# Self attention of a decoder layer: the denominators of all four head groups summed on VectorE, the last group finished inside the output projection, and one feed-forward block moved to the last cross attention

## The chip, the cores and the metric

The kernel runs on one core of one Trainium2 chip. The metric is the device time of one execution in microseconds (us); the figure quoted is the median of three runs. The engines are called TensorE (PE in the profile, PEld for its weight loads), VectorE (DVE), ScalarE (ACT), GpSimd (POOL) and SyncE (SP, which issues the DMAs). TensorE writes its results into PSUM; everything else lies in SBUF.

## What is computed

The reference is one pre-norm decoder layer on four batches of 512 tokens with 512 features, 16 heads of 32, all in float32:

```python
x = x + attn(layernorm(x), q_w, q_b, k_w, k_b, v_w, v_b, o_w, o_b)   # causal self attention
x = x + xattn(layernorm(x), ctx, ctx)     # causal, raw queries, keys and values, no weights
x = x + ffn(layernorm(x), W_up, W_down, W_gate, W_expert)
```

Both attentions are a softmax over the earlier positions. The feed-forward part is `relu(f @ W_up.T) @ W_down.T` plus `f @ W_expert` times the sum of a softmax over the two largest gate values of eight.

## The kernel before, in words

The kernel goes through the batches b = 0 to 3 one after the other. Activations are kept transposed in tiles of 128 x 4 x 512 (`NC` = 4 chunks of 128 features). The 16 heads are treated in four **groups** g of four heads (`HG` = 4): a group is one chunk of 128 features, and its four heads use four quarters of TensorE, either of its rows or of its columns. Keys are cut into four blocks j of 128; block j concerns the queries from 128 j on, so a block (g, j) is 512 - 128 j wide.

**One attention** has two phases. `with_maxima` computes all scores once to find the row maxima (matmul `sm`, ScalarE copy `s`, GpSimd mask, VectorE reduction), in ten units, with matmuls of other work spread in between as `fill`. `attend` computes the transposed scores with the maxima subtracted (`sc`), lets ScalarE take the exponentials and GpSimd cut the triangle, and multiplies by the values (`values`, `shares`, result in `pv`). It has ten units of 512 columns; units may hold two pieces. In order, for groups 2 and 3, the pieces are (2,0); (2,3) with (2,1); (2,2) with (3,2); (3,0); (3,3) with (3,1). The values of a unit are issued two units after its scores.

The softmax's **denominator** is had in one of two ways. A group in `self.added` has its exponentials added up by VectorE (`add_up`, line 510) in a tile `sum`, and only four matmuls with ones (`summed`, line 516) sum that over the partitions, into the second half of a `pv` pair. Any other group has a second matmul with ones for each value matmul (the loop over `u` in `shares`, line 462). In self attention groups 0, 1 and 2 are added and group 3 is not; in cross attention groups 0 and 2 are. From the denominator VectorE makes the inverse (`inverse`, called by `spread`: transpose at line 537, reciprocal at 539, transpose at 540), and the output is multiplied by it (`scale`, on GpSimd at line 532, or at once on VectorE at line 501 for group 3).

`shares` also places these steps. In the kernel before, the denominator of group 2 goes into a pair of its own (`ls_s`), issued with the values of (3,0); its inverse and its multiplication come with the last values of group 3, followed by the inverse and multiplication of group 3.

**After a self attention** `out_projection` multiplies the four chunks c of the output `oT` by the output weights (`pm_o`, line 687, four matmuls of 512 for each c) into two PSUM pairs. Between the chunks stand `sides`: the two transpositions of the context (`tp_c`), and, in b = 0 to 2, the two of the next batch's normalised input (`tp_a`), in the order c=0, `tp_c`, `tp_a`, c=1, `tp_c`, c=2, `tp_a`, c=3. After c=1 `behind` issues four scans on VectorE (line 672) with a memset each on GpSimd. Then VectorE adds the result to x and normalises (`tp_q` transposes that), while TensorE does two steps of other work. In b > 0, GpSimd adds the output bias to x (line 588) between the attention and the projection.

**PSUM** has eight banks, used as four *pairs* (tile tag `ps`, two banks each). Each of `sm`, `sc`, `pv`, `ls`, `pm`, `tp` takes a pair.

**SBUF** tiles are shared by tag: `sum` uses the tiles `ck_t` and `beh_t` in turn, which the context and the scans use later.

**The order** on TensorE, VectorE, ScalarE and GpSimd is the order of the program (`manual_schedule`); each engine works through its queue in that order and waits where an operand isn't there. SP's DMAs are placed by the framework.

**The fills.** The feed-forward part of a batch is cut into `gates` (two steps), `ups`, `downs` and `experts` (four blocks of four matmuls each), which fill phases of the next batch: for batch 2, `ups[:2]` go into the self maxima of batch 3, and the other two, the gates and the downs, into its cross attention (`between_self`, `between_cross`).

Of the kernel before, what the change touches and what calls it, by code (L numbers as in the profile page):

```python
# [11 lines left out]
AF = mybir.ActivationFunctionType  # L12
ALU = mybir.AluOpType
# [13 lines left out]
def decoder_layer(  # L27
# [21 lines left out]
    nc = tc.nc  # L49
    B, S, D = x.shape  # L50
# [3 lines left out]
    NC = D // P  # L54
# [10 lines left out]
    def pair(name):  # L65

        return ps.tile([P, 2, S], F32, tag="ps", name=name)
# [194 lines left out]
    class Attention:  # L262
        def __init__(self, q_t, k_t, v, cross, name):
            self.q_t, self.k_t, self.v, self.cross, self.name = q_t, k_t, v, cross, name
            self.nm, self.mrow, self.pv, self.out = {}, {}, {}, None
            self.more, self.sums, self.rden, self.e = {}, {}, {}, None
            self.added = (0, 2) if cross else range(NC - 1)

        def maxima(self, pieces):

# [179 lines left out]
        def shares(self, g, blocks):  # L450

            js = {j for j, *_ in blocks}
            first = js == {0} if g % 2 == 0 else js == {2}
            last = js == {2} if g % 2 == 0 else 1 in js
            if first:
                self.pv[g] = pair(f"pv_{self.name}_{g}")
            pv = self.pv[g]
            for u in range(1 if g in self.added else 2):
                for n, (j, c, pts) in enumerate(blocks):
                    for r in range(HG):  # L460
                        h = g * HG + r
                        nc.tensor.matmul(  # L462
                            pv[r * HD : (r + 1) * HD, u, j * P :],
                            lhsT=ones if u else self.v[:, j, h * HD : (h + 1) * HD],
                            rhs=pts[r // 2][:, r % 2, c : c + S - j * P],
                            start=first,
                            stop=last and n == len(blocks) - 1,
                            skip_group_check=True,
                        )
            if self.cross:  # L470


                if (first if g == 1 else js == {0}) and g - 1 in self.added:
                    self.summed(g - 1, self.pv[g - 1])
                    self.divide(g - 1)
                elif js == {0} and g > 0:
                    self.scale(g - 1)
                if 1 in js and g == NC - 1:
                    self.scale(g - 1)
                if last and g not in self.added:  # L480
                    self.divide(g)
                    if g == NC - 1:
                        self.scale(g)
                return
            if first and g == 0:
                self.out = act.tile([P, NC, S], F32, tag="o_t", name=f"oT_{self.name}")
            if (first if g in self.added else js == {0}) and g - 1 in self.added:
                self.sum_in = pv if g in self.added else pair(f"ls_{self.name}")
                self.summed(g - 1, self.sum_in)
            if js == {0} and g - 2 in self.added:  # L490
                self.scale(g - 2)
            if 1 in js and g - 1 in self.added and g not in self.added:
                self.spread(g - 1, self.sum_in)
                self.scale(g - 1)
            if last and g in self.added:
                nc.scalar.copy(self.out[:, g, :], pv[:, 0, :])
                if g > 0:
                    self.spread(g - 1, pv)
            elif last:
                num, den = pv[:, 0, :], pv[:, 1, :]  # L500
                nc.vector.tensor_tensor(
                    self.out[:, g, :], num, self.inverse(g, den), ALU.mult
                )

        def add_up(self, made):
            for g, j, c, pts in made:
# [21 lines left out]

        def scale(self, g):
            o = self.out[:, g, :]  # L530
            engine = nc.vector if self.cross and g == NC - 1 else nc.gpsimd
            engine.tensor_tensor(o, o, self.rden.pop(g), ALU.mult)

        def inverse(self, g, den):
# [132 lines left out]
    def behind(e, c):  # L667

        if c == 0:
            e.beh_t = act.tile([P, NC, S], F32, tag="beh_t", name=f"behT_{e.b}")  # L670
        nc.gpsimd.memset(e.beh_t[:, c, S - 1 : S], 0.0)
        nc.vector.tensor_tensor_scan(
            e.beh_t[:, c, S - 2 :: -1],
            e.ck_t[:, c, S - 1 : 0 : -1],
            zero.to_broadcast([P, S - 1]),
            0.0,
            ALU.add,
            ALU.add,
        )

    def out_projection(e, a, sides):

        b = e.b
        pms = [pair(f"pm_o{b}_{n}") for n in range(2)]
        for c in range(NC):
            for t in range(NT):
                nc.tensor.matmul(  # L687
                    pms[t // 2][:, t % 2, :],
                    lhsT=a.out[:, c, t * P : (t + 1) * P],
                    rhs=wo_sb[:, c, :],  # L690
                    start=(c == 0),
                    stop=(c == NC - 1),
                )
            if c < NC - 1:
                run(sides[c::3])
            if c == 1:
                for g in range(NC):
                    behind(e, g)

        def add(t):  # L700
            xi = e.x[:, t, :]
            nc.vector.tensor_tensor(xi, pms[t // 2][:, t % 2, :], xi, ALU.add)

        made, norms = layernorms(lambda t: e.x[:, t, :], f"q{b}", add)
        run(norms)
        return made
# [33 lines left out]
    def ffn(e):  # L740
        b, f_t, made = e.b, e.f_t, {}

        def up(f):
            if f == 0:
                made["h"] = act.tile(
                    [P, NC, S], F32, tag="o_t" if b != B - 2 else "f_t", name=f"hT_{b}"
                )
            if f % 2 == 0:
                made["u"] = pair(f"pm_u{b}_{f}")
            yield from project_t(made["u"][:, f % 2, :], wup_sb, f_t, f)  # L750
            if f % 2 == 1:
                nc.scalar.activation(made["h"][:, f - 1 : f + 1, :], made["u"], AF.Relu)

        def share():
# [99 lines left out]
    def run(steps):  # L854
        for step in steps:
            for _ in step() or ():
                pass
# [55 lines left out]
    def attend(a, late):  # L913


        units = []
        for g in range(0, NC, 2):
            units += [[(g, 0)], [(g, 3), (g, 1)], [(g, 2), (g + 1, 2)]]
            units += [[(g + 1, 0)], [(g + 1, 3), (g + 1, 1)]]
        waiting, held, todo = [], [], []  # L920

        def values():
            made = waiting.pop(0)
            a.values(made)

            if len(made) > 1 and made[0][1] == 2:
                held.append(made[1:])
            elif waiting and waiting[0][0][1] > 0:
                if made[0][1] == 0 and held:
                    a.add_up(held.pop())  # L930
                a.add_up(waiting[0] if waiting[0][0][1] == 3 else waiting[0][:1])

        for n, pieces in enumerate(units):
            waiting.append(a.scores(pieces))
            if n in late:
                for copy in a.rows(late[n]):
                    copy(nc.scalar.copy)
            if a.cross and n in (5, 7):
                todo.append(a.masked(n // 2))
            if n in (6, 9) and todo:  # L940
                todo.pop(0)()
            if len(waiting) > 2:
                values()
        while waiting:
            values()

    with tc.manual_schedule(engines=BY_HAND):
        e, norms, turns = norm_in(0, x0)
# [8 lines left out]
        between_self = query_key(e) + value(e)  # L957
        skip, between_cross, ahead = 4, [], []
        for b in range(B):
# [11 lines left out]
            made = out_projection(e, sa, context(e) + turns)  # L971
# [15 lines left out]
            made = add_cross(e, ca)  # L987
# [8 lines left out]
            gates, ups, downs, experts = ffn(e)  # L996
            if b + 3 < B:
                between_self, between_cross = gates[:1] + ups + gates[1:] + downs, experts
            elif b + 2 < B:
                between_self, between_cross = gates[:1] + ups + gates[1:] + downs, []  # L1000
                ahead = experts
            elif more:
                between_self, ahead = ahead + ups[:2], experts
                between_cross = gates[:1] + ups[2:] + gates[1:] + downs
            else:
                run(gates[:1] + ups + gates[1:])
                run(downs[:2] + experts[:2] + downs[2:] + experts[2:])
# [51 lines left out]
```

## Time and profile before

| | |
|---|---|
| median of three runs | 809.82 us (809.55 to 809.85) |
| profiled execution | 809.92 us |
| its span, first to last instruction | 808.2 us |
| granted TensorE clock | 1.00 |
| one self attention, `attend` (b = 1) | 250.79 to 280.91, 30.12 us |
| its output projection up to the cross maxima | 280.91 to 310.39, 29.48 us |
| the same in b = 3 | 653.66 to 679.15, 25.49 us |
| TensorE's waits for others, all that are listed | 1.7 + 1.5 + 0.9 + 0.8 + 0.8 + 0.6 + 0.3 us |

Times inside the profile count from the start of the span. A line of a timeline gives start, duration, engine, line of the kernel, instruction, tile written and tiles read, their shapes, how many instructions were merged, and in brackets how long the engine was idle before and what ended that. On TensorE one float32 matmul shows as two records, and successive records overlap, since matmuls are pipelined: the distance from start to start is the price, not the duration. `pv_s` is a self attention's `pv`, `pv_c` a cross attention's, and so on.

### The profile page before, as it was taken

The numbers are of one execution on the slowest core, as the hardware profiler recorded it, in microseconds if no ns is written. First come the engines' busy times: TensorE is split into PE (matmuls) and PEld (weight loads), VectorE is DVE, ScalarE is ACT, GpSimd is POOL, SyncE is SP. The second block draws the span as 40 slices with busy tenths as digits, with TensorE's granted clock in tenths as the row PEclk, the third lists the DMA queues.
The fourth block names the chain that finished last, engine by engine and source line by source line (L and its number), as shares of the span: only waits on it lengthen the run. The fifth ranks groups of instructions, "written<-read, shape, count | busy, mean of one in ns | idle before, by whom it ended". The sixth has DMA issues, their size and how long they took to land. (4 is left out here: it accounts for less than half of the span.)

```text
span 808.2 us, 13950 instructions
## 1 busy us (share of the span) xinstructions
PE 796.8 (99%) x5616; PEld 379.9 (47%) x5616; DVE 563.7 (70%) x957; ACT 395.4 (49%) x448; POOL 332.8 (41%) x523
## 2 busy tenths in 40 slices
PE   8999999999999999999999999999999999999998
PEld 7444454444444454444544445444444454434444
DVE  2478865879678854588867786688859766988512
ACT  2457526861546515566045752686056824674110
POOL 4334612554234732266333482266423653465100
PEclk9999999999999999999999999999999999999999
DMA  9601000001001000020100000000102000000101
GB/s 337 236 28 28 1 1 1 2 2 53 1 27 27 2 1 0 2 77 29 53 14 14 1 2 1 0 2 1 54 26 79 2 2 0 1 2 2 52 1 52
DMA packets 13680, 24.50 MB, mean 30 GB/s; under 512 B 1968, under 2 KB 2224, under 8 KB 13616
## 3 DMA queue, kind: packets, MB, share of 16 engines
q1 hardware_dynamic: 13184, 22.96, 8.4%
q8 instruction: 44, 0.72, 0.4%
q10 hardware_dynamic: 432, 0.66, 0.2%
q14 instruction: 20, 0.16, 0.1%
HBM read 19.42 MB, written 4.19 MB: 29 GB/s over the span
## 5 line engine op out<-in xcount | busy, mean ns | idle before, releaser
L317 DVE TENSOR_REDUCE nm_s<-s_s 128x2 f32<-128x1024 f32 (+3 forms) x128 | 97.0, 811 | 35.2 <-POOL s_s L305 35.2
L317 DVE TENSOR_REDUCE nm_c<-s_c 128x2 f32<-128x1024 f32 (+3 forms) x128 | 95.8, 810 | 31.0 <-POOL s_c L305 31.0
L297 ACT COPY s_s<-sm_s 128x1024 f32<-128x1024 f32 x80 | 77.1, 1015 | 70.7 <-PE sm_s L286 36.4
L297 ACT COPY s_c<-sm_c 128x1024 f32<-128x1024 f32 x80 | 77.1, 1016 | 35.9 <-PE sm_c L286 16.2
L305 POOL TENSOR_SCALAR_AFFINE_SELECT s_c<-s_c 128x512 f32<-128x512 f32 (+1 forms) x80 | 43.9, 550 | 100.4 <-ACT s_c L297 100.4
L305 POOL TENSOR_SCALAR_AFFINE_SELECT s_s<-s_s 128x512 f32<-128x512 f32 (+1 forms) x80 | 43.8, 551 | 97.1 <-ACT s_s L297 97.1
L423 ACT ACTIVATE pt_c<-sc_c 128x1024 f32<-128x1024 f32 x64 | 61.7, 1031 | 21.0 <-PE sc_c L400 15.4
L510 DVE TENSOR_TENSOR sum_s<-sum_s,pt_s 128x256 f32<-128x256 f32 (+2 forms) x72 | 59.8, 895 | 16.7 <-PE pv_s L462 16.7
L431 POOL TENSOR_SCALAR_AFFINE_SELECT pt_c<-pt_c 128x512 f32<-128x512 f32 (+1 forms) x64 | 51.1, 806 | 27.0 <-ACT pt_c L423 26.6
L223 PE MATMUL pm_d<-wdown_sb,hT 128*128 128x512 f32 x128 | 61.5, 610 | 0.0
L423 ACT ACTIVATE pt_s<-sc_s 128x1024 f32<-128x1024 f32 x56 | 53.9, 1030 | 12.6 <-PE sc_s L400 7.0
L235 PE MATMUL pm_u<-fT,wup_sb 128*128 128x512 f32 x128 | 59.3, 604 | 0.0
L223 PE MATMUL pm_v<-wv_sb,xnT 128*128 128x512 f32 x128 | 58.8, 600 | 0.0
L687 PE MATMUL pm_o<-wo_sb,oT_s 128*128 128x512 f32 x128 | 57.8, 596 | 0.0
L235 PE MATMUL pm_qk<-xnT,wk_sb 128*128 128x512 f32 x120 | 57.3, 607 | 0.0
L389 PE MATMUL sc_c<-cqT,ckT 32*128 32x384 f32 (+3 forms) x512 | 56.0, 464 | 1.4 <-ACT sum_c L423 0.8
L235 PE MATMUL pm_qk<-xnT,wq_sb 128*128 128x512 f32 x120 | 56.7, 604 | 0.0
L223 PE MATMUL pm_e<-wexp_sb,fT 128*128 128x512 f32 x120 | 56.3, 604 | 0.0
L389 PE MATMUL sc_s<-qT,kT 32*128 32x128 f32 (+3 forms) x512 | 54.4, 462 | 1.2 <-ACT sum_s L423 0.9
L431 POOL TENSOR_SCALAR_AFFINE_SELECT pt_s<-pt_s 128x512 f32<-128x512 f32 (+1 forms) x56 | 48.1, 868 | 17.6 <-ACT pt_s L423 17.0
L286 PE MATMUL sm_c<-ckT,cqT 32*128 32x512 f32 (+3 forms) x512 | 47.5, 460 | 0.0
L286 PE MATMUL sm_s<-kT,qT 32*128 32x512 f32 (+3 forms) x512 | 47.0, 461 | 0.0
(164 smaller groups left out, 1269.3 us busy)
## 6 DMA issues: line engine op xcount, KB each, us to landing
cv<-in_ctx_dram SPq DMA_DIRECT2D x16, 256.0 KB, 4.0
out_dram<-x SPq DMA_DIRECT2D x15, 256.0 KB, 2.0
x<-in_x_dram SPq DMA_DIRECT2D x14, 256.0 KB, 4.1
xin<-in_x_dram SPq DMA_DIRECT2D x12, 256.0 KB, 2.7
wq_sb<-in_wq_dram SPq DMA_DIRECT2D x2, 512.0 KB, 6.2
wk_sb<-in_wk_dram SPq DMA_DIRECT2D x2, 512.0 KB, 7.8
wv_sb<-in_wv_dram SPq DMA_DIRECT2D x1, 1024.0 KB, 8.3
wo_sb<-in_wo_dram SPq DMA_DIRECT2D x1, 1024.0 KB, 9.7
```

The costliest lines, as they stand in the source:

```text
L223: nc.tensor.matmul(pm, lhsT=lhs_t[:, c, t * P : (t + 1) * P], rhs=w[:, c, :], start=(c == 0), stop=(c == NC - 1),)
L235: nc.tensor.matmul(pm, lhsT=w[:, c, f * P : (f + 1) * P], rhs=rhs_t[:, c, :], start=(c == 0), stop=(c == NC - 1),)
L286: nc.tensor.matmul(scs[r // 2][:, r % 2, c : c + (i + 1) * P], lhsT=self.q_t[h, g, i * P : (i + 1) * P], rhs=self.k_t[h, g, : (i + 1) * P] ...
L297: nc.scalar.copy(s, scs[n])
L305: nc.gpsimd.affine_select(out=diagonal, in_=diagonal, compare_op=ALU.is_ge, fill=NEG, base=0, pattern=[[0, 2], [0, len(pieces)], [-1, P]], ...
L317: nc.vector.tensor_reduce(self.nm[g][:, i, 2 * n : 2 * n + 2], made[n][:, :, c : c + (i + 1) * P], axis=AX.X, op=ALU.max, negate=True,)
L389: nc.tensor.matmul(scs[r // 2][:, r % 2, c : c + S - j * P], lhsT=self.k_t[h, g, j * P : (j + 1) * P], rhs=self.q_t[h, g, j * P :], start= ...
L423: nc.scalar.activation(pt, scs[n], AF.Exp)
L431: nc.gpsimd.affine_select(out=diagonal, in_=diagonal, compare_op=ALU.is_ge, fill=0.0, base=0, pattern=[[0, 2], [0, len(pieces)], [1, P]], ...
L510: nc.vector.tensor_tensor(to, to, pts[n][:, :, c : c + S - j * P], ALU.add)
L687: nc.tensor.matmul(pms[t // 2][:, t % 2, :], lhsT=a.out[:, c, t * P : (t + 1) * P], rhs=wo_sb[:, c, :], start=(c == 0), stop=(c == NC - 1),)
```

## The change

Self attention adds group 3 up as well. `self.added` covers all four groups, so `shares` issues no matmul with ones there. The denominator of group g-1 is always issued right after the first value matmuls of group g (`first`), into the second half of group g's `pv`; the pair `ls_s` within the attention is gone, and group 3's output is copied by ScalarE like the others. The inverse of group 2 comes with the last values of group 3, and its multiplication (GpSimd) at the end of `attend`. A new method `finish` is called in `out_projection` after c=1 and its `sides`, ahead of `behind`: it takes a pair, issues the denominator of group 3, its inverse, and its multiplication on VectorE.

The fourth `sum` uses the tile `beh_t`, which `behind` writes next.

Separately, for batch 2, one feed-forward block `up` moves from the self maxima of batch 3 to its cross attention, and the four `up` blocks of that batch take a pair and a Relu of their own instead of one for two.

```diff
-            self.added = (0, 2) if cross else range(NC - 1)
+            self.added = (0, 2) if cross else range(NC)
...
-            if (first if g in self.added else js == {0}) and g - 1 in self.added:
-                self.sum_in = pv if g in self.added else pair(f"ls_{self.name}")
-                self.summed(g - 1, self.sum_in)
-            if js == {0} and g - 2 in self.added:
+            if first and g > 0:
+                self.summed(g - 1, pv)
+            if js == {0} and g > 1:
                 self.scale(g - 2)
-            if 1 in js and g - 1 in self.added and g not in self.added:
-                self.spread(g - 1, self.sum_in)
-                self.scale(g - 1)
-            if last and g in self.added:
+            if last:
                 nc.scalar.copy(self.out[:, g, :], pv[:, 0, :])
                 if g > 0:
                     self.spread(g - 1, pv)
-            elif last:
-                num, den = pv[:, 0, :], pv[:, 1, :]
-                nc.vector.tensor_tensor(
-                    self.out[:, g, :], num, self.inverse(g, den), ALU.mult
-                )
+
+        def finish(self):
+
+            ls = pair(f"ls_{self.name}")
+            self.summed(NC - 1, ls)
+            self.spread(NC - 1, ls)
+            self.scale(NC - 1)
...
-            engine = nc.vector if self.cross and g == NC - 1 else nc.gpsimd
+            engine = nc.vector if g == NC - 1 else nc.gpsimd
...
             if c == 1:
+                a.finish()
                 for g in range(NC):
                     behind(e, g)
...
+        alone = b == B - 2
+
...
-            if f % 2 == 0:
+            if f % 2 == 0 or alone:
                 made["u"] = pair(f"pm_u{b}_{f}")
             yield from project_t(made["u"][:, f % 2, :], wup_sb, f_t, f)
-            if f % 2 == 1:
+            if alone:
+                nc.scalar.activation(made["h"][:, f, :], made["u"][:, f % 2, :], AF.Relu)
+            elif f % 2 == 1:
                 nc.scalar.activation(made["h"][:, f - 1 : f + 1, :], made["u"], AF.Relu)
...
         while waiting:
             values()
+        if not a.cross:
+            a.scale(NC - 2)
...
-                between_self, ahead = ahead + ups[:2], experts
-                between_cross = gates[:1] + ups[2:] + gates[1:] + downs
+                between_self, ahead = ahead + ups[:1], experts
+                between_cross = gates[:1] + ups[1:] + gates[1:] + downs
```

## The prediction

> **What bounds the kernel now.** I read the page's engine totals first, then the list of waits for TensorE, then the timelines of TensorE, VectorE and GpSimd around the end of one self attention (third batch, b=2), then the same stretch of the last batch (b=3).
>
> ```profile
> PE 796.8 (99%) x5616; PEld 379.9 (47%) x5616; DVE 563.7 (70%) x957; ACT 395.4 (49%) x448; POOL 332.8 (41%) x523
> ```
>
> TensorE is busy nearly throughout, and the waits listed for it come to under 8 us. So TensorE's queue sets the time: a matmul that leaves it is a gain, and a new wait in it is a loss of the same size. The end of the self attention, on TensorE (start, duration, instruction; matmuls overlap, so I price by the distance between starts):
>
> ```profile
> 473.12 1.07 PE L462 MATMUL pv_s<-pt_s,v 128*32 128x256 f32 x16
> 474.00 0.61 PE L462 MATMUL pv_s<-pt_s,ones 128*32 128x256 f32 x8
> 474.43 1.04 PE L462 MATMUL pv_s<-pt_s,v 128*32 128x512 f32 x8
> 475.29 1.04 PE L462 MATMUL pv_s<-pt_s,ones 128*32 128x512 f32 x8
> 476.15 1.04 PE L516 MATMUL ls_s<-sum_s,ones 128*32 128x512 f32 x8
> 477.01 1.05 PE L462 MATMUL pv_s<-pt_s,v 128*32 128x128 f32 x16
> 477.87 1.05 PE L462 MATMUL pv_s<-pt_s,ones 128*32 128x128 f32 x16
> 478.85 3.70 PE L687 MATMUL pm_o<-wo_sb,oT_s 128*128 128x512 f32 x8
> 482.39 1.04 PE L251 MATMUL tp_c<-ident,cv 128*128 128x128 f32 x8
> 483.26 1.04 PE L251 MATMUL tp_a<-ident,xn_a 128*128 128x128 f32 x8
> ```
>
> The three rows with "pt_s,ones" are the work to be removed; "ls_s" is group 2's denominator. VectorE and GpSimd in the same stretch:
>
> ```profile
> 469.87 5.71 DVE L510 TENSOR_TENSOR sum_s<-sum_s,pt_s 128x256 f32<-128x256 f32 x6
> 475.58 0.72 DVE L537 STREAM_TRANSPOSE dt_s<-pv_s 128x512 f32<-128x512 f32 x1
> ...
> 476.62 0.71 DVE L540 STREAM_TRANSPOSE dt_s<-rden_s 128x512 f32<-128x512 f32 x1
> ```
>
> ```profile
> 470.03 1.44 POOL L532 TENSOR_TENSOR oT_s<-oT_s,dt_s 128x512 f32<-128x512 f32 x1
> ...
> 480.45 4.97 POOL L588 TENSOR_TENSOR x<-x,bo_sb 128x512 f32<-128x512 f32 x4
> ```
>
> The six adds that complete group 2's sum end at 475.58. TensorE reads that sum at 476.15, 0.57 us later. The cover is thin, and the change shifts exactly this read. The four batches show the same stretch to 0.05 us.
>
> **The change, part by part.**
>
> *Removed.* Group 3's ones matmuls: 474.43-474.00 = 0.43, 476.15-475.29 = 0.86, and the last pair 0.87 (half of 478.85-477.01, less 0.1 for the switch back to 128 columns, which stays). Together -2.15 us of TensorE per batch.
>
> *Added on TensorE.* `finish` has one denominator of four matmuls, between a transposition and an output-projection step. The nearest row is the gate's `lg` at L759 (same 128*32 by 512 form, same neighbours): 669.34 to 670.34 is 1.00, and the next eight matmuls take 3.53 instead of 3.43. So +1.09. Group 2's denominator keeps its 0.86. Work alone: -1.06 per batch, -4.2 in all.
>
> *Where group 2's denominator goes.* It stood behind the values of piece (3,0); now it is issued as soon as group 3's first piece (3,2) is done, that is at 474.00, where the first ones row began. Its last operand is ready at 475.58. Nothing before that point in VectorE's queue changes, so TensorE waits 1.6 us. Behind it in TensorE's queue stand the values of (3,0) and (3,3),(3,1) and the whole output projection, and everything waits. If TensorE could use the first half of the sum (pairs of heads 0 and 1, complete some 0.9 us sooner) while the second is added, 0.8 would be left. Bounds 0.75 to 1.7; I take 1.6, because all four matmuls must have run before the row quarters are free for the next set. The output projection then starts at 478.85-2.15+1.6 = 478.3.
>
> *VectorE.* Six more adds per batch for group 3. They wait for the values of (3,0) (about 477.4) and follow group 1's inverse, which ends at 477.33. The like rows are 5.71 for six, and 4.57 for the six before them in the queue that ran with less beside them; I take 5.4, to 482.8. One 256-element add takes 0.41 alone and 1.49 beside GpSimd's 1.44 multiply, and here group 1's multiply of 1.28 lies beside the adds. The Trainium skill, page "SBUF — State Buffer", section "Who interferes with whom", says that a VectorE instruction with two SBUF inputs and a GpSimd one that reads SBUF lock each other out for whole instructions; by it the six would take the 4.57 of the earlier row and 1.28 on top, 5.9, an estimate; the inverse would move back by 0.5. Then group 2's inverse (0.72+0.25+0.71 and gaps, 1.75) starts at 482.8, where today the inverses are over by 480.8.
>
> *PSUM.* There are four pairs. Pair `pv` of group 3 now carries group 2's denominator and is free only after that inverse's first transposition, 483.5. The output projection holds two pairs, `tp_c` takes the last, and `tp_a` (0.87 us behind it) finds none: it is due at 478.3+3.54+0.87 = 482.7, and the next pair comes at 483.5 (`pv`) or at 483.9 (`tp_c`, copied by ScalarE 1.2 after its matmuls). A wait of 0.8 to 1.2, in the three batches that have a `tp_a`; I take 1.0, bounds 0 to 1.3. A page of the skill points the same way: "Perfetto Trace Analysis", section "Optimization Strategy", reads a gap that repeats on the engine that should be saturated as a possible lack of SBUF or PSUM for the next tile. No such gap shows before the change.
>
> *Group 3's finish.* Its inverse and multiply (1.75+0.69) run while TensorE does step c=2 (3.44): hidden, with 1 us to spare; without that cover 2.4. Group 2's multiply on GpSimd ends about 485.9 and is needed at c=2, after 489: hidden. Behind it stand the bias adds, then over by 490.9; the first sum that reads them comes after 495: hidden. No DMA is moved, so SP's queue is as before. The ScalarE copy of group 3 (0.59) is needed only at c=3: nothing.
>
> *The scans.* VectorE's four scans (4.56) used to start when `ckT` was copied; now they stand behind `finish`, and their memsets on GpSimd behind the bias adds of 4.97, which themselves move back with group 2's multiply. In b=0 to 2 the next `tp_q` comes 6.9 us after the projection: covered. In b=3 the cover is only `lg` and one feed-forward block:
>
> ```profile
> 663.62 4.56 DVE L672 TENSOR_TENSOR_SCAN behT<-ckT,zero 128x511 f32<-128x511 f32 x4 [7.28 <-ACT ckT L257]
> 668.10 0.67 DVE L702 TENSOR_TENSOR x<-pm_o,x 128x512 f32<-128x512 f32 x1
> ...
> 673.13 0.52 DVE L206 TENSOR_SCALAR xn_q<-x,mv_q,rs_q 128x512 f32<-128x512 f32 x1
> ```
>
> ```profile
> 673.87 1.04 PE L251 MATMUL tp_q<-ident,xn_q 128*128 128x128 f32 x8
> ```
>
> Today the second normalised tile is done at 673.65, 0.2 before its use. After: the denominator ends at 662.8, inverse and multiply at 665.3, scans 665.5 to 670.1, so everything behind them is 2.0 later, at 675.6, while `tp_q` is due at 674.4. A wait of 1.3 with the handover, bounds 0.4 to 2.2.
>
> *The moved block.* Four matmuls (3.44) go from the last self maxima (24 to 20) to the last cross maxima (17 to 21); TensorE's sum is the same. The donor loses cover: cross maxima of b=0 and b=2, with 20 and more VectorE work, take 30.99 without a visible stall, so 0. The receiver now takes 29.96 (679.15 to 709.11). By the 30.99, less four matmuls (3.44) and a row turn (0.3), plus the gate's 0.9, it should take 28.15. So 1.8 are stalls, one of them in
>
> ```profile
> 705.28 1.98 PE L286 MATMUL sm_c<-ckT,cqT 32*128 32x512 f32 x8
> ```
>
> against 1.14 for its equals. Four more matmuls give ScalarE and VectorE time, but the gate's PSUM pair is held a block longer. I take -1.1, bounds -1.8 to 0. Splitting the Relu into four is ScalarE work with gaps around it (49% busy): nothing; uncovered, 0.5.
>
> *Sum.* b=0 to 2: -1.06+1.6+1.0 = +1.54 each, 4.6. b=3: -1.06+1.6+1.3-1.1 = +0.7. Together +5.3 on the profiled execution's 809.92 (span 808.2 and 1.7 around it), which stands 0.1 above the median 809.82: 815.2.
>
> **The rivals.**
> 1. *Only the denominator waits; a PSUM pair is free for `tp_a`.* For it: three of four pairs are free when the projection starts. Against: I count all four in use at `tp_a`. 815.2-3.0 = 812.2.
> 2. *Halves overlap too* (0.8 instead of 1.6, no PSUM wait): 812.2-3.2 = 809.0, no change.
> 3. *Faster: VectorE is ready in time.* One mechanism, at the first read of group 2's sum: if the six adds end by 474.0 instead of 475.58, TensorE runs straight through and only the removed matmuls and the last cross count: -4.2-1.1+0.9 (the scans in b=3 remain) = -4.4, 805.4. It decides where the waits of a batch fall below the 1.06 saved. For it: the preceding six adds took 4.57, not 5.71. Against: that gains 1.1 of 1.6, and their queue is fixed until then.
> 4. *The moved block does nothing*, the last cross stalls as before: 816.3.
>
> **How the numbers follow.** Forecast with rival 4: 0.62; rival 1: 0.14; rival 2: 0.09; rival 3: 0.15. All high bounds together (0.1x4+0.3x3+0.9+1.1) add 3.3; I close at 818.0. The low end takes in rival 2 and leaves out rival 3: 808.5. Faster by over 0.2% (about what a measurement of this kernel can tell from no change): 0.15; within: 0.09; slower: 0.76.
>
> **What would show it.** In the changed profile: TensorE stands about 1.6 us at the denominator written to `pv_s` in front of the values of (3,0), waiting for VectorE L510, in each batch; `tp_a` starts over 0.8 after `tp_c` ends in three batches; `tp_q` of the last batch starts over 5.5 after the projection; the last cross maxima take near 32. The forecast is wrong if the first of these waits is under 0.5, or if `tp_a` follows `tp_c` at once.

## The result, and the profile after

The changed kernel takes 813.2 us (median of six runs, 813.09 to 813.58) against 809.79 (809.55 to 809.87): ratio 1.004, 95% interval 1.0029 to 1.0052, or 3.4 us slower. The profiled execution took 813.16 us, with a span of 811.5.

The page's engine totals after:

```profile
PE 796.9 (98%) x5520; PEld 375.9 (46%) x5520; DVE 583.0 (72%) x981; ACT 398.4 (49%) x454; POOL 334.1 (41%) x523
```

TensorE executes 96 records fewer and is busy as long as before, in a span 3.3 us longer. VectorE has 24 more instructions, the adds of group 3 in four batches.

TensorE's timeline at the end of the self attention of the third batch (start, duration, instruction, and in brackets the idle time listed before it):

```profile
474.16 1.07 PE L462 MATMUL pv_s<-pt_s,v 128*32 128x256 f32 x16
475.64 1.66 PE L514 MATMUL pv_s<-sum_s,ones 128*32 128x512 f32 x6 [0.41 <-DVE sum_s L508]
476.69 0.62 PE L462 MATMUL pv_s<-sum_s,v 128*32 128x512 f32 x2
477.13 0.60 PE L514 MATMUL pv_s<-sum_s,ones 128*32 128x512 f32 x2
...
479.38 3.70 PE L685 MATMUL pm_o<-wo_sb,oT_s 128*128 128x512 f32 x8
482.92 1.04 PE L251 MATMUL tp_c<-ident,cv 128*128 128x128 f32 x8
483.80 1.04 PE L251 MATMUL tp_a<-ident,xn_a 128*128 128x128 f32 x8
...
489.07 1.07 PE L514 MATMUL ls_s<-sum_s,ones 128*32 128x512 f32 x8
490.07 3.70 PE L685 MATMUL pm_o<-wo_sb,oT_s 128*128 128x512 f32 x8
```

VectorE beside it:

```profile
470.91 5.71 DVE L508 TENSOR_TENSOR sum_s<-sum_s,pt_s 128x256 f32<-128x256 f32 x6
476.63 0.72 DVE L535 STREAM_TRANSPOSE dt_s<-pv_s 128x512 f32<-128x512 f32 x1
...
478.31 4.74 DVE L508 TENSOR_TENSOR sum_s<-sum_s,pt_s 128x512 f32<-128x512 f32 x6
482.98 0.70 DVE L535 STREAM_TRANSPOSE dt_s<-pv_s 128x512 f32<-128x512 f32 x1
```

The denominator of group 2 comes up behind the first values of group 3, at 474.16 + 0.89 = 475.05. VectorE ends the sum at 476.63. The listed idle time of 0.41 is only the part before the first two heads; the other two start when the second half of the sum is there, and the row's 1.66 hides that. The distance of starts gives the true loss: from the first of these rows to the output projection it is 5.22 us, against 5.73 before, although 2.15 us of matmuls are gone. So 1.64 us are waited.

Then `tp_a` follows `tp_c` at once (483.80 after 482.92 + 0.87). VectorE's first transposition of group 2's inverse, which frees the PSUM pair of group 3, ends at 483.68: 0.1 us earlier.

By phase, from the starts of the first matmuls of each: the attention (`attend`) is shorter by 0.50 to 0.52 in every batch. The stretch from the projection to the cross maxima is longer by 1.19 in the first three batches (30.67 against 29.48) and by 2.09 in the last (27.58 against 25.49). The last self maxima take 32.45 (33.99), the last cross maxima 32.75 (29.96), and the last cross attention up to the transpositions `tp_x` 37.03 (37.98).

TensorE's wait in the last self maxima, and in front of the last cross attention:

```profile
618.16 1.98 PE L235 MATMUL pm_u<-fT,wup_sb 128*128 128x512 f32 x4 [1.39 <-DVE x L833]
...
623.38 0.40 PE L349 MATMUL mt_s<-identb,parts 128*128 128x128 bf16 x4 [0.26 <-DVE parts L343]
```

```profile
674.72 0.60 PE L251 MATMUL tp_q<-ident,xn_q 128*128 128x128 f32 x4
675.79 0.66 PE L251 MATMUL tp_q<-ident,xn_q 128*128 128x128 f32 x4 [0.47 <-DVE xn_q L206]
```

VectorE at the same place:

```profile
675.22 0.51 DVE L206 TENSOR_SCALAR xn_q<-x,mv_q,rs_q 128x512 f32<-128x512 f32 x1
```

The moved block left the self maxima 3.44 us of matmuls shorter, but they are shorter by 1.54 only: `pm_u` waits for a PSUM pair that an expert block holds until VectorE has weighed it (L833), and VectorE is behind with its reductions. And the first two tiles of `tp_q` take 1.66 (674.72 to 676.38) instead of 0.87: the first runs at once, the second waits for its normalised tile, which VectorE (the last line) ends at 675.73.

### The profile page after: what moved, and what is told of

Same layout as the page of the kernel before. It is cut to its first block, busy times and chain, and to the rows that moved or that the text cites. A ratio compares the mean times of both kernels' runs of the same rounds, so it can differ in the third digit from the quotient of the medians.

```text
span 811.5 us, 13787 instructions
## 1 busy us (share of the span) xinstructions
PE 796.9 (98%) x5520; PEld 375.9 (46%) x5520; DVE 583.0 (72%) x981; ACT 398.4 (49%) x454; POOL 334.1 (41%) x523
## 5 line engine op out<-in xcount | busy, mean ns | idle before, releaser
L508 DVE TENSOR_TENSOR sum_s<-sum_s,pt_s 128x256 f32<-128x256 f32 (+2 forms) x96 | 78.8, 885 | 15.2 <-PE pv_s L462 15.2
L423 ACT ACTIVATE pt_s<-sc_s 128x1024 f32<-128x1024 f32 x48 | 46.2, 1032 | 7.1 <-PE sc_s L400 7.1
L431 POOL TENSOR_SCALAR_AFFINE_SELECT pt_s<-pt_s 128x512 f32<-128x512 f32 x48 | 39.5, 829 | 16.2 <-ACT pt_s L423 15.5
```

The source lines that it names most:

```text
L423: nc.scalar.activation(pt, scs[n], AF.Exp)
L431: nc.gpsimd.affine_select(out=diagonal, in_=diagonal, compare_op=ALU.is_ge, fill=0.0, base=0, pattern=[[0, 2], [0, len(pieces)], [1, P]], ...
L508: nc.vector.tensor_tensor(to, to, pts[n][:, :, c : c + S - j * P], ALU.add)
```

## The experiments

All but the ninth are medians of five to eleven executions, with the kernel before run beside them; its median in the three sets was 809.72, 809.72 and 809.78. The diffs are against the changed kernel, and "..." marks what is left out.

**1. The attention part alone.**

```diff
-                between_self, ahead = ahead + ups[:1], experts
-                between_cross = gates[:1] + ups[1:] + gates[1:] + downs
+                between_self, ahead = ahead + ups[:2], experts
+                between_cross = gates[:1] + ups[2:] + gates[1:] + downs
...
-        alone = b == B - 2
+        alone = False
```

> The change without the moved feed-forward block (two blocks in the last self maxima again, one pair and one Relu for two). Theory A, the attention part carries the loss: in the changed kernel each batch's attend is 0.5 us shorter and its output projection 1.2 longer (2.1 in the last batch), +3.6 in all, and the moved block nets +0.3 (+1.9 of stalls in the last self maxima, -1.6 in the last cross). So about 812.9, 3.1 above before; the last self maxima take 33.99 again and the last cross maxima about 30. Theory B, the block is most of the loss (its stall of 1.9 in the donor without a return): 811.3.

Measured: 812.8, ratio 1.0039 (1.0026 to 1.0051). The last self maxima are back at 33.99 and the last cross maxima at 29.96. The loss is in the attention part: 3.1 of 3.4 us.

**2. The moved block alone**, put into the kernel before.

> The kernel before with the moved block alone. Theory A: donor +1.9 (a stall of 1.4 where pm_u waits for a PSUM pair that VectorE L829 frees late, and 0.4 at the row turn), receiver -1.6: 810.1, within 0.5 of before. Theory B: +1.9 and no return, 811.7. The forecast's own step (no stall in the donor, -1.1 in the receiver): 808.7.

Measured: 810.22, ratio 1.0009 (1.0 to 1.0018). The list of waits for TensorE names the same stall as in the changed kernel:

```profile
PE pm_u L235 <- DVE x L831: 1.4, 1, 1.4
```

The last self maxima take 32.46, which is 1.91 over what is left of them (33.99 - 3.44). The last cross maxima and attention give back 1.60: (33.40 - 32.75) + (37.98 - 37.03), where 33.40 is the 29.96 of before and the block's 3.44. The block opens a stall where it is taken away and fills one where it goes. The move was not tried apart from the four pairs and Relus that come with it.

**3. Group 2's denominator one piece later.**

```diff
-            if first and g > 0:
+            if (js == {0} if g == NC - 1 else first) and g > 0:
                 self.summed(g - 1, pv)
```

> The change with one thing moved: the denominator of group 2 is issued behind the values of (3,0), as in the kernel before, into the same pair. Theory A, TensorE's wait for VectorE's sum is what eats the saving: the wait falls from 1.6 to about 0.7 us per batch (TensorE comes 0.86 later, VectorE ends when it did), so 813.2 - 4x0.87 = 809.7. Theory C, the wait only moves on to the next late thing (the last exponentials, cut by GpSimd 1.2 us after TensorE needs them): 813.2 - 4x0.4 = 811.6 or no change at all.

Measured: 812.98, ratio 1.0043 (1.003 to 1.0055): as slow as the change. But the wait did shrink. TensorE's timeline of the third batch:

```profile
476.01 1.39 PE L514 MATMUL pv_s<-sum_s,ones 128*32 128x512 f32 x6
...
478.62 3.70 PE L685 MATMUL pm_o<-wo_sb,oT_s 128*128 128x512 f32 x8
482.16 1.04 PE L251 MATMUL tp_c<-ident,cv 128*128 128x128 f32 x8
483.82 1.09 PE L251 MATMUL tp_a<-ident,xn_a 128*128 128x128 f32 x8 [0.63 <-DVE dt_s L535]
```

The projection starts at 478.62 instead of 479.38 (0.85 sooner, counted from the start of the attention), and `tp_a` at 483.82 instead of 483.80, now 1.66 after `tp_c` instead of 0.87. What was gained is waited for again in front of `tp_a`, and the releaser is L535, the transposition that frees group 3's pair. Neither theory on record had named this place; the forecast had.

**4. The first chunk of the projection ahead of the last values.** The four matmuls of c=0 and then group 2's denominator stand in front of the values of (3,3),(3,1). `ahead` issues c=0, and `out_projection` goes on with c=1.

```diff
-            if first and g > 0:
+            if first and 0 < g < NC - 1:
                 self.summed(g - 1, pv)
...
             pv = self.pv[g]
+            if last and g == NC - 1 and not self.cross:
+                self.summed(g - 1, pv)
...
         while waiting:
+            if ahead and len(waiting) == 1:
+                ahead()
             values()
```

> The change with the first chunk of the output projection (four matmuls, 3.44 us) issued ahead of group 2's denominator and of the last values, so that TensorE has work while VectorE ends the sum. Theory A: the wait of 1.6 us per batch goes, two more switches between 128 and 32 columns cost 0.2: 813.2 - 4x1.4 = 807.6, 2.2 below before. Theory C (the tail is bound by VectorE's and GpSimd's own chain up to the cross attention): the wait shows up again at c=2 or at tp_q, and the time stays above 811.

Measured: 813.04, ratio 1.0044 (1.0031 to 1.0056). TensorE's waits list no denominator any more; in its place stands

```profile
PE tp_a L251 <- DVE dt_s L537: 3.2, 3, 1.1
```

and in the timeline of the third batch

```profile
480.02 1.06 PE L516 MATMUL pv_s<-sum_s,ones 128*32 128x512 f32 x8
480.91 1.05 PE L464 MATMUL pv_s<-pt_s,v 128*32 128x128 f32 x16
481.88 1.09 PE L251 MATMUL tp_c<-ident,cv 128*128 128x128 f32 x8
484.04 1.09 PE L251 MATMUL tp_a<-ident,xn_a 128*128 128x128 f32 x8 [1.07 <-DVE dt_s L537]
```

`tp_a` comes 2.16 after `tp_c` instead of 0.87: 1.29 us, which is the wait of 1.64 that was taken away, less 0.35 for the chunk's new place (see experiment 6). Theory A fell in both runs, since up to `tp_a` the stretch hangs on VectorE's chain. From this came theory D: the two waits are one chain at two places.

**5. `tp_a` behind c=2**, nothing else.

```diff
-                run(sides[c::3])
+                run(sides[2:] if c == NC - 2 else sides[c : c + 1])
```

> The change with one thing moved: both transpositions of the next batch (tp_a) stand behind c=2, so that no tp_a follows the first tp_c. Theory D (formed after the earlier runs): TensorE's wait at group 2's denominator and the wait of tp_a for the PSUM pair that group 2's inverse frees are two places on one chain of VectorE; whichever comes first hides the other. In the change the first is 1.6 us and the pair comes 0.1 us before tp_a asks for it, so moving tp_a alone gives nothing: 813.2, within 0.3. Theory E (the two add up, as the forecast had it): about 3 less, 810.2.

Measured: 813.3, ratio 1.0043 (1.0029 to 1.0058). Alone it gives nothing either; in the changed kernel there was no wait of `tp_a` to take away.

**6. Experiments 4 and 5 together.**

> The first chunk of the projection ahead of the last values, and tp_a behind c=2 as well. Theory D: now neither wait is left; in each of the three batches with a tp_a the 1.3 us go that tp_c's row showed over its 0.87 in the kernel with the first chunk ahead: 813.0 - 3x1.35 = 809.0. In the last batch tp_q still waits, about 1.6. Theory C (VectorE's chain is late everywhere up to the cross attention, and the wait turns up at c=2 or c=3 next): no gain, 812 to 813.

Measured: 809.14, ratio 0.9995 (0.9986 to 1.0004). Two edits that each give nothing give 4 us together, as theory D has it. In each of the first three batches the stretch from the attention's start to `tp_q` takes 53.72, against 55.01 in the change and 54.32 before. TensorE in the third batch:

```profile
472.44 1.10 PE L464 MATMUL pv_s<-sum_s,v 128*32 128x512 f32 x8
473.47 3.70 PE L685 MATMUL pm_o<-wo_sb,oT_s 128*128 128x512 f32 x8
477.10 1.07 PE L516 MATMUL pv_s<-sum_s,ones 128*32 128x512 f32 x8
477.98 1.05 PE L464 MATMUL pv_s<-pt_s,v 128*32 128x128 f32 x16
478.96 1.09 PE L251 MATMUL tp_c<-ident,cv 128*128 128x128 f32 x8
479.89 3.60 PE L685 MATMUL pm_o<-wo_sb,oT_s 128*128 128x512 f32 x8
```

No row waits. What this order is worth per batch is thus 0.6 us (54.32 - 53.72), not the 1.06 of the forecast. The matmuls alone save 0.96 (2.15 less 1.19); the other 0.35 is lost around the chunk that now stands between blocks of 32 columns: the values ahead of it take 1.03 from start to start instead of 0.86, and the chunk 3.63 instead of 3.54.

**7. Both, the block back, and one more block ahead of the first `tp_q` of the last batch.** Beside the edits of 1, 4 and 5:

```diff
-            run(steps[:2])
+            run(steps[: 2 if more else 3])
             norm_cross(e, made, 0)
-            run(steps[2:3])
+            run(steps[2 if more else 3 : 3])
```

> The kernel of the run before, with the feed-forward block moved back, and in the last batch one more block of other work ahead of the first tp_q (three steps, then both halves of tp_q). Theory D: 809.0, less 0.4 for the block, less up to 1.6 for tp_q: 807.0, 2.7 below before; that is 4x1.0 of matmuls saved less the switches. If tp_q waits for something other than the scans, which stand in front of it on VectorE, 808.6.

Measured: 807.21, ratio 0.9969 (0.9957 to 0.9981): faster than both kernels, 2.5 us below the one before and 6.0 below the change.

**8. The last step of 7 alone**, in the change.

> The change with one more block of other work ahead of the first tp_q of the last batch, nothing else. If tp_q waits there because the scans stand in front of the layer norm on VectorE, the 0.8 of its row over 0.87 goes: 813.2 - 0.8 = 812.4. If it waits for something that moves along with the block (PSUM, or a ScalarE copy), the wait shows up at the second half of tp_q and the time stays at 813.2.

Measured: 812.55, ratio 1.0035 (1.0022 to 1.0047), 0.65 below the change. All four tiles of the last `tp_q` now run in one piece:

```profile
671.17 7.13 PE L235 MATMUL pm_u<-fT,wup_sb 128*128 128x512 f32 x16
678.14 1.91 PE L251 MATMUL tp_q<-ident,xn_q 128*128 128x128 f32 x16
```

So the wait was for time on VectorE, not for something that moves along with the block.

**9. Group 2's inverse held back 1.4 us** by two transpositions into a tile that nobody reads, in the change. One execution only.

> The change with VectorE held up by two extra transpositions (1.4 us, into a tile that nobody reads) in front of group 2's inverse. Theory D: the pair comes 1.4 later, tp_a must take the pair of tp_c instead and starts about 1.1 late in three batches: 813.2 + 3.3 = 816.5, plus nothing in the last. If tp_a did not depend on that pair: 813.2, since the inverse itself is needed only at c=2, 4 us later.

Measured: 818.6, with a span of 816.9. TensorE's waits:

```profile
PE tp_a L252 <- ACT ckT L258: 3.3, 3, 1.1
```

`tp_a` does not wait for the late inverse: it takes the pair of `tp_c` as soon as ScalarE has copied it (ckT), as the working in the forecast had it, and the three batches take 1.32 more each (56.33 against 55.01). The last batch loses 1.06 on top, 0.36 in the attention and projection and 0.70 at `tp_q`. GpSimd's multiply of group 2 and the bias adds behind it come later, and group 3's multiply on VectorE now lies beside the last of them and takes 1.73 instead of 0.69:

```profile
669.50 1.73 DVE L534 TENSOR_TENSOR oT_s<-oT_s,dt_s 128x512 f32<-128x512 f32 x1
```

```profile
665.73 4.96 POOL L590 TENSOR_TENSOR x<-x,bo_sb 128x512 f32<-128x512 f32 x4
```

So the output that c=3 reads is late, and the scans start 1.04 later after the projection's start. Of the rest of the 5.4 in the spans, 0.4 lies before the first attention. The expectation had left the last batch out.

**10. As 7, with the block left where the change has it.**

> First chunk of the projection ahead, tp_a behind c=2, one more block ahead of the last tp_q, and the feed-forward block left where the change has it, in the last cross attention. By the comparison of the change with and without the moved block: 807.2 + 0.4 = 807.6. If the block had been there to fill the stalls of the last cross attention and the fuller kernel needed it, it would be below 807.2.

Measured: 807.94, ratio 0.9976 (0.9967 to 0.9985). The block doesn't help the fuller kernel: it costs 0.7 against experiment 7.

## Why the prediction was right, and where its steps were not

*Work alone, -1.06 per batch.* Nearly right in size: -0.96. The ones matmuls are gone, and the new denominator costs 1.00 and 0.19 in its neighbours, 1.19 in all where 1.09 was forecast (0.10 had been counted for the one behind it, 0.09 went to the one ahead of it).

*The wait at group 2's denominator, 1.6.* Right: 1.64 in each batch, at the place named, for the adds named. The whole wait of 1.6 was paid, not the 0.8 of the second rival, although the profile lists 0.4 as idle. The reason given for 1.6 (all four matmuls must have run before the next set) is not what the trace shows. TensorE did use the first half of the sum, from 475.64 on. But the values of the first two heads stand behind the denominators of the other two in the queue, which wait for the end of the sum at 476.63; they start at 476.69, before the last of those denominators at 477.13.

*`tp_a`'s wait for a PSUM pair, 1.0 in three batches.* Wrong in the changed kernel: 0. The prediction had named this as a sign that it is wrong (`tp_a` follows `tp_c` at once), and this step failed. The term behind it was mis-sized: six adds of group 3 at 5.4, measured 4.74. They were priced between two rows of 4.57 and 5.71, both with GpSimd's masks beside them; here only one multiply lay beside them. With 4.74 the prediction's own sum gives the pair at 482.9 and `tp_a` at 482.7; the adds also began 0.14 sooner than worked out. The pair came 0.1 us before it was asked for. Experiments 3, 4 and 9 show that the step's mechanism exists, down to the second source of a pair; it was only 0.1 us short of being seen. The first rival (denominator alone, 812.2) has the structure that came out.

*`tp_q` in the last batch, 1.3.* Right in kind, 0.8 in size, and 0.9 with what follows up to the cross maxima. The scans start when the inverse and multiply end, and the additions and the layer norm follow without a gap:

```profile
665.72 4.55 DVE L670 TENSOR_TENSOR_SCAN behT<-ckT,zero 128x511 f32<-128x511 f32 x4
670.19 0.67 DVE L701 TENSOR_TENSOR x<-pm_o,x 128x512 f32<-128x512 f32 x1
```

In this trace the stretch lies 0.2 later as a whole, so 665.72 is the 665.5 of the forecast, and `tp_q`, at 674.72, came only 0.1 later than the 674.4. The second tile is ready at 675.73 where, with the 0.2, 675.8 was forecast. The mistake is in what needs that tile: not the start of `tp_q`, as the prediction had it, but its second four transpositions, due 0.43 later. That holds for the kernel before too, where the cover was 0.65 (673.65 for a use at 674.30) and not 0.2. Experiment 8 shows the cause of the wait: with other work in front of `tp_q` it is gone.

*The moved block: 0 in the donor, -1.1 in the receiver.* The donor was wrong: +1.9. The comparison was with a cross phase of 20 matmuls (30.99), where the fill is queries and keys, which ScalarE takes out of PSUM. The last self maxima are filled with expert blocks, which VectorE takes out, and the wait there names VectorE (L833). The receiver gave 1.6: 0.65 in the cross maxima and 0.95 in the cross attention behind them. The prediction had looked at the maxima alone; why the attention is shorter was not tried. Together +0.3 instead of -1.1, and experiment 2 measures +0.5.

*The sum.* Three batches at -0.51+1.19 = 0.68 instead of 1.54 are 2.6 less. The last batch has 0.68 + 0.9 + 0.3 = 1.9 instead of 0.7. Together 3.9 where 5.3 was forecast. The spans differ by 3.3: 0.3 lies before the first attention, where such a difference also shows between kernels that are equal there, and 0.3 behind the last instruction of VectorE: from its end to the end of the span it is 2.83 or 2.84 in every kernel with four sums, and 3.14 and 3.19 in the two without. The cause of this last 0.3 was not tried.

The direction was right since the deciding wait was right. That the size came within 2.0 us (815.2 forecast, 813.2 measured) is in part luck: the 3.0 for `tp_a` were not there and 0.4 of `tp_q`'s wait neither, while the moved block cost 1.4 more than forecast and the work with its wait 0.14 more in each batch. The first rival's 812.2 is the nearer number.

## What to carry to other kernels

On an engine that works through its queue in order, a matmul that is removed is worth its time only if what stands behind it is ready that much sooner: look up when the last operand of each later read is written, here 0.57 us ahead of its use. Waits that hang on one chain of another engine need not add up, and need not show one by one. Here the first hid the next: moving either reader alone gave nothing (813.04 and 813.3), and both together gave 4 us (809.14). The way out was not less work but other work in the gap (a projection chunk whose operand was long ready), and asking for the scarce PSUM pair later.

## What the runs showed of the hardware that was not expected

GpSimd's multiply of group 1, which lies beside the new adds, took 1.62 us instead of its 1.28, and the longest add 1.77 (a like one took 0.68 in the kernel before):

```profile
478.47 1.62 POOL L530 TENSOR_TENSOR oT_s<-oT_s,dt_s 128x512 f32<-128x512 f32 x1 [1.35 <-DVE dt_s L538]
```

```profile
L508 DVE TENSOR_TENSOR sum_s<-sum_s,pt_s x96: 409/898/1766, 73.0 to 656.0; 128x256 f32<-128x256 f32 x32, 128x768 f32<-128x768 f32 x32, 128x512 f32<-128x512 f32 x32
```

(Durations in ns, least, median and most.) The Trainium skill, page "SBUF — State Buffer", section "SBUF: two separate sides", has whichever of a VectorE instruction with two SBUF inputs and a GpSimd one that reads SBUF starts first hold their shared pair of ports for its whole instruction, and the other blocked until then. The rows agree. In the third batch the second add starts at 478.88, inside the multiply, and ends at 480.64, 0.55 after the multiply's end; the multiply, which started inside the first add, lost 0.34. In experiment 9 VectorE's multiply starts at 669.50, inside the last bias add, and ends at 671.23, again 0.54 after the end of GpSimd's row (1.73 us; 0.69 in the change, where it starts behind the bias adds). Yet all six adds took 4.74 us, far from the 5.9 that the estimate from that rule gave: it had put the multiply on top of a row of 4.57 that was already slowed by GpSimd's masks (an add of 768 elements took up to 1.38 there and 0.94 here).
